# A two-layer graph and expert network on one core: input statistics, the epsilon and a bookkeeping part placed ahead of the choice of experts

## The chip, the cores and the metric

The kernel runs on 1 core of one Trainium2 chip. The metric is the device time of one execution in microseconds (us). Below, TensorE is PE in the profile, VectorE is DVE, ScalarE is ACT, GpSimd is POOL, and SP is the queue that issues most of the DMAs.

## The reference

The input `x` has 128 graphs of 64 nodes with 256 features (8192 rows in all), and `adj` holds a 64x64 matrix for each graph. All is float32. Two layers follow each other, and each has a graph part and an expert part. Cut to what matters here, the first layer is:

```python
# graph part of layer 0, on xn = layernorm(x)
agg = epsilon * xn + einsum('bnm,bmd->bnd', adj, xn)
h   = silu(rmsnorm(agg @ W1 + b1) * rms_weight)      # 256 -> 1024
x   = x + h @ W2 + b2                                # 1024 -> 256
# expert part of layer 0, on xn = layernorm(x)
top, idx = top_k(xn @ gate_w.T, 6)                   # 6 of 64 experts for each row
w   = softmax(top)
mix = sum over the 6 of w_k * (xn @ lattice[idx_k])  # each expert is a 256x256 matrix
x   = x + layernorm(xn + mix @ out_w.T + out_b)
```

The second layer has another graph part and 8 experts with a hidden layer of 512, of which each row uses 2.

## The kernel before

**Passes.** The program is a row of stages. The first pass computes the graph part of layer 0 and the routing of its experts; its scatters write each row, once for each of its six experts, into a table in DRAM that is ordered by expert. Then come the pages of the 64 experts, a second pass with the rest of layer 0 and the graph part of layer 1, and the pages of the 8 experts. The change lies in the first pass.

**Tiling.** A block is 256 rows, held as two tiles of 128 partitions; there are 32 blocks. The pass is a software pipeline. A list names pairs of a lag and a function, and `staggered` walks through it: in step s each function works on block s minus its lag, in the list's order. So in step s the hidden layer of block s is computed (lag 0), the input of block s+1 is normalised (lag -1), block s-2 gets its residual (lag 2), block s-3 is routed (lag 3), and the rest of the rows of block s-4 are sent (lag 4).

**What sets the order.** TensorE, VectorE and ScalarE run under a manual schedule: each executes its own instructions in the order in which the list emits them, one after the other, so an instruction that waits holds up all behind it on its engine. SP's DMAs are ordered by the framework. GpSimd issues the scatters in the order in which they are written.

**The functions of a step that the change and the prediction speak of.**

- `norm_a` (lag -1): the statistics of the input block, on VectorE, two pairs of L45 and L46 (one pair for each tile). They read the block that `load0` (lag -2, L620 for the rows and L574 for the adjacency) had loaded in an earlier step.
- `norm_e` (lag -1): adds epsilon times the unit matrix to the adjacency (L656, VectorE).
- `norm_s` (lag -1): the reciprocal root of that variance on ScalarE (L58 a logarithm, L59 an exponential). `norm_b` then normalises the block on VectorE (L666), and `aggregate` multiplies with the adjacency on TensorE (L674) and copies the result with ScalarE (L677).
- `residual_a` (lag 2): adds the input to the projected block (L723, VectorE) and takes the statistics of the sum (again L45 and L46). `residual_s` has the root of it (L58, L59, ScalarE). `residual_b` makes a small shift (L733, VectorE) and writes the normalised rows six times (L736, ScalarE); two DMAs store them (L738, L739).
- `hidden` (lag 0): four parts of the product with W1 on TensorE (L684), each followed by squares on ScalarE (L687). `square_sum` adds the squares (L694, VectorE), `rms` makes the mean with a matmul (L698) and its reciprocal root on ScalarE, and `scale` applies it (L706 on VectorE, L708 on ScalarE).
- `project` (lag 1): the product with W2 (L717, TensorE). `turn` and `gate` (lag 2): the transposes of the normalised rows (L76) and the logits of the 64 experts (L752).
- `choose` (lag 3): the six largest logits and a one-hot mark for each (L204 to L209, VectorE). `count` (lag 3) adds up the marks on TensorE (L217), `weigh` prepares the weights (L283 and L285 on VectorE, L286 on ScalarE), and `place` turns the counts into rows of the table (L300 to L327, VectorE).
- `keep_books` (lag 3, from block 4 on): the bookkeeping of the table's chunks on VectorE, spread over four steps (reach, grow, and two of note), and in each step in two parts, half 0 and half 1 (L228 to L267).
- `send` (lags 3 and 4): for each of the six ranks a weight on VectorE (L305) and two scatters by GpSimd (L334).
- `load_lattice` (lag 1): a load of expert matrices in some of the steps (L787).

In ScalarE's order of a step stand the squares of the first two hidden parts, the root of `residual_s`, the root of `norm_s`, the exponential of `weigh`, the squares of the other two hidden parts, the rows of L736, the copies of L677 and L746, and the root and the scaling of the hidden layer.

Of the kernel before, what the change touches and what calls it, by code (L numbers as in the profile page):

```python
# [485 lines left out]
def staggered(n, stages, first=0):  # L486

    for s in range(first + min(lag for lag, _ in stages), n + max(lag for lag, _ in stages)):
        for lag, f in stages:
            if first <= s - lag < n:  # L490
                f(s - lag)
# [3 lines left out]
def two_layer_gnn_moe_kernel(ctx: ExitStack, tc: tile.TileContext, a: dict, out: bass.AP):  # L495
# [84 lines left out]
    r0 = Router(tc, const, small, dram, N, D, E0, K0, T, P, 14 * P, 4, "r0", 3)  # L580
# [23 lines left out]
    with tc.tile_pool(name="c0", bufs=1) as c0, \  # L604
# [12 lines left out]
        def load0(b):  # L617
            B = blocks[b]
            B["x"] = x = x_view[:, b % 4 * T:(b % 4 + 1) * T, :]
            nc.sync.dma_start(out=x, in_=by_tile(x_in[ts(b, C), :]))  # L620
            B["at"] = load_adjacency(b)
# [57 lines left out]
        def hidden(b, j):  # L679
            B = blocks[b]  # L680
            B["ph", j] = ph = ph_pool.tile([P, 2, C], F32, name="ph")
            for c in range(2):
                for k in range(KD):
                    nc.tensor.matmul(ph[:, c, :], lhsT=w1[:, k, ts(2 * j + c, P)], rhs=B["aggT"][:, k, :],  # L684
                                     start=(k == 0), stop=(k == KD - 1))
            for c in range(2):
                nc.scalar.activation(sq[:, 2 * j + c, :], ph[:, c, :], AF.Square,  # L687
                                     bias=b1[:, 2 * j + c:2 * j + c + 1], scale=1.0)
# [87 lines left out]
        def send(b, k):  # L776

            B = blocks[b]
            r0.release(k, *B["w"], B["xs"])
            r0.send(B["row"], B["xs"], b > LOOK, (k,))  # L780

        def load_lattice(b):
# [5 lines left out]

        nc.scalar.preload_act_table_set("natural_log_exp_and_others")
        staggered(NB, (  # L790
            (3, choose),
            (3, lambda b: r0.keep_books(b, 0)),
            (2, residual_a),
            (4, lambda b: send(b, 2)),
            (-2, lambda b: load0(b) if b > 1 else None),
            (-1, norm_a),
            (0, lambda b: hidden(b, 0)),
            (0, lambda b: hidden(b, 1)),
            (2, residual_s),
            (-1, norm_s),  # L800
            (-1, norm_e),
            (4, lambda b: send(b, 3)),
            (3, weigh),
            (0, lambda b: hidden(b, 2)),
# [474 lines left out]
```

## Time and profile before

| what | us |
|---|---|
| median of 3 runs | 2058.91 |
| lowest and highest of them | 2055.96 and 2059.22 |
| the profiled execution | 2052.92 |
| its span, from the first instruction to the last | 2051.1 |
| TensorE's mean granted clock in it | 0.974 |
| the first pass in that span, to the last table scatter | 0 to about 645 |

The profile is of one execution. Its page gives the busy time of each engine and the span in 40 slices of 51 us, in tenths of busy time. The windows view gives the same sums for a chosen stretch. The list of waits says for each engine and line what it waited for, in total, how often, and the longest. The timeline gives each instruction's start and duration; a bracket after it is the idle time of the engine before it and what ended that. Where two neighbours on an engine don't depend on each other, the next one's start lies a little before the end of the one in front, so the time that an instruction takes out of its engine is read from start to start.

### The profile page before, as it was taken

To read this page: it belongs to the slowest core of one execution; us is meant where nothing else is said; L and a number is where in the kernel's file an instruction comes from. 1 tells how busy PE (TensorE), PEld (TensorE's weight loads), DVE (VectorE), ACT (ScalarE), POOL (GpSimd) and SP (SyncE) were. 2 spreads that over 40 slices of the span, in tenths; PEclk is the share of its full clock that TensorE was granted. 3 is DMA by queue.
4 is the path that set the end of the run, shared out by engine and by line. 5 is a ranking of instruction groups with operands and counts; after the bars stand their busy time and mean duration, and the time that the engine had idled before them with its cause. 6 is when DMAs were issued, how large, how long until landed. Compare 5 with 4: busy or idle time off the path is not lost. (4 is left out here: it accounts for less than half of the span.)

```text
span 2051.1 us, 37214 instructions
## 1 busy us (share of the span) xinstructions
PE 1923.0 (94%) x10516; PEld 1678.1 (82%) x10516; DVE 1200.0 (59%) x4205; ACT 1018.1 (50%) x2033; POOL 1162.0 (57%) x1134
## 2 busy tenths in 40 slices
PE   6999999999966989999999799999989999999996
PEld 5888888888865778888877688888868888888885
DVE  5899999999975333344333389999862222222221
ACT  4888888888851222222222266666643333333332
POOL 1377667677677777777777723333343444444443
PEclk9999999999977999999999899999989999999998
DMA  4244555544476988666665799888527766666664
GB/s 123 80 143 148 168 165 170 169 159 141 133 267 206 309 252 267 214 207 207 207 207 171 266 362 338 267 278 278 190 92 172 178 162 162 162 163 163 163 163 86
DMA packets 282561, 397.91 MB, mean 194 GB/s; under 512 B 56025, under 2 KB 236393, under 8 KB 282353
## 3 DMA queue, kind: packets, MB, share of 16 engines
q1 hardware_dynamic: 202880, 246.61, 40.2%
q0 software_dynamic: 64416, 136.14, 22.1%
q10 hardware_dynamic: 15056, 12.69, 1.9%
q8 instruction: 94, 1.54, 0.3%
q14 instruction: 115, 0.93, 0.2%
HBM read 222.84 MB, written 176.64 MB: 195 GB/s over the span
## 5 line engine op out<-in xcount | busy, mean ns | idle before, releaser
L334 POOL DMA_INDIRECT r0x<-xs,r0row x384 | 402.1, 1047 | 236.0 <-DVE lat L706 72.2
L341 POOL DMA_INDIRECT r0y<-px x404 | 393.3, 973 | 123.3 <-DMA r0y<-px 49.7
L918 PE MATMUL py<-lat,pxT 128*128 x1616 | 389.4, 384 | 18.7 <-ACT pxT L905 15.4
L351 POOL DMA_INDIRECT out_x<-py_s,px x138 | 214.6, 1555 | 293.8 <-DMA out_x<-py_s,px 125.9
L922 DVE TENSOR_SCALAR px<-py,px 128x256 f32<-128x256 f32 x404 | 177.0, 480 | 309.6 <-PE py L918 303.9
L918 PEld LDWEIGHTS py<-lat,pxT 128*128 128x128 f32 x1616 | 294.3, 192 | 59.3 <-ACT pxT L905 20.4
L905 ACT COPY pxT<-pt 128x512 f32<-128x512 f32 x202 | 117.9, 585 | 368.6 <-PE pt L903 252.7
L1217 ACT ACTIVATE phid<-ph,pw 128x256 f32<-128x256 f32 x276 | 130.6, 473 | 323.2 <-issue 213.9
L1215 PE MATMUL ph<-pxT,pw 128*128 128x256 f32 x1104 | 251.3, 381 | 0.7 <-ACT pxT L1206 0.7
L1235 PE MATMUL py<-fw,phid 128*128 (+1 forms) x1104 | 249.7, 379 | 0.0
L717 PE MATMUL ps<-lat 128*128 128x256 f32 x1024 | 238.5, 382 | 0.0
L1215 PEld LDWEIGHTS ph<-pxT,pw 128*128 128x128 f32 x1104 | 210.9, 191 | 30.0 <-ACT pxT L1206 1.1
L684 PE MATMUL ph<-lat 128*128 128x256 f32 x1024 | 232.2, 386 | 2.7 <-DVE lat L706 2.0
L1235 PEld LDWEIGHTS py<-fw,phid 128*128 128x128 f32 x1104 | 204.5, 190 | 25.0
L684 PEld LDWEIGHTS ph<-lat 128*128 128x128 f32 x1024 | 195.1, 193 | 29.4 <-issue 2.4
L334 POOL DMA_INDIRECT r1x<-xs,r1row x128 | 127.7, 998 | 160.9 <-DVE r1run L313 47.0
L717 PEld LDWEIGHTS ps<-lat 128*128 128x128 f32 x1024 | 193.8, 192 | 24.9
L1229 DVE TENSOR_SCALAR p<-p 128x2 f32<-128x2 f32 x69 | 12.8, 186 | 225.5 <-ACT p L1228 225.5
L1238 DVE TENSOR_TENSOR py_s<-py,pb 128x512 f32<-128x512 f32 x69 | 47.7, 692 | 154.9 <-PE py L1235 152.7
L903 PE MATMUL pt<-ident,px 128*128 128x128 f32 x808 | 125.3, 276 | 11.6 <-DMA px<-r0x 11.3
L903 PEld LDWEIGHTS pt<-ident,px 128*128 128x128 f32 x808 | 100.4, 142 | 37.7 <-DMA px<-r0x 8.9
L994 PE MATMUL ps<-ident,y 128*128 128x128 f32 x768 | 94.7, 281 | 16.1 <-DMA y<-r0y 16.1
(303 smaller groups left out, 2980.4 us busy)
## 6 DMA issues: line engine op xcount, KB each, us to landing
px<-r0x SPq DMA_DIRECT2D x404, 129.0 KB
y<-r0y SPq DMA_DIRECT2D x64, 768.0 KB
pw<-in_L_ffn_W1b SPq DMA_DIRECT2D x69, 514.0 KB
px<-r1x SPq DMA_DIRECT2D x69, 258.0 KB
x<-x SPq DMA_DIRECT2D x64, 256.0 KB
pb<-in_L_ffn_b SPq DMA_DIRECT2D x69, 128.0 KB
r0x<-r0filler ACTq DMA_DIRECT2D x64, 129.0 KB
lat<-in_x SPq DMA_DIRECT2D x32, 256.0 KB
```

Source lines behind the costliest of these rows:

```text
L334: i = self.nc.gpsimd.indirect_dma_start(out=self.table[:, :], out_offset=bass.IndirectOffsetOnAxis(ap=row[:, t, k:k + 1], axis=0), in_=xs[ ...
L341: d = self.nc.gpsimd.indirect_dma_start(out=self.answer[:, :], out_offset=bass.IndirectOffsetOnAxis(ap=x[:, self.D:self.D + 1].bitcast(I32 ...
L351: i, d = f"{self.name}add{i}", self.nc.gpsimd.indirect_dma_start(out=self.total[:, :], out_offset=bass.IndirectOffsetOnAxis(ap=x[:, self.D ...
L684: nc.tensor.matmul(ph[:, c, :], lhsT=w1[:, k, ts(2 * j + c, P)], rhs=B["aggT"][:, k, :], start=(k == 0), stop=(k == KD - 1))
L717: nc.tensor.matmul(B["po"][:, t, :], lhsT=B["hT"][:, c, ts(t, P)], rhs=w2[:, c, :], start=False, stop=(t == T - 1 and c == KH - 1))
L903: nc.tensor.transpose(pt[:, k, ts(q, P)], Q["px"][:, q, ts(k, P)], ident)
L905: nc.scalar.copy(xT[:, :, :n * P], pt[:, :, :n * P])
L918: nc.tensor.matmul(py[:, q, :], lhsT=xT[:, k, ts(q, P)], rhs=lat[:, ds(regs["e"][(2 * j + q) % 4], 1), k, :].rearrange("p o d -> p (o d)") ...
L922: nc.vector.tensor_scalar(px[:, q, :D], py[:, q, :], px[:, q, D + 1:D + 2], None, op0=ALU.mult)
L1215: nc.tensor.matmul(ph, lhsT=w[:, k * F1 + c * P:k * F1 + (c + 1) * P], rhs=Q["xT"][:, k, :], start=(k == 0), stop=(k == KD - 1))
L1217: nc.scalar.activation(hid[:, c, :], ph, AF.Relu, bias=w[:, KD * F1 + c:KD * F1 + c + 1], scale=1.0)
L1235: nc.tensor.matmul(py[:, t, :], lhsT=Q["hid"][:, c, ts(t, P)], rhs=fw2[:, ds(e, 1), c, :].rearrange("p o d -> p (o d)"), start=(c == 0), s ...
```

## The change

In the list of the first pass three entries change their place. `norm_a` and `norm_e`, which stood behind `residual_a`, now stand at the head of the list, and the first half of `keep_books` now stands ahead of `choose` instead of behind it. The functions themselves are as they were, and so are all other entries. On VectorE a step's order is now the input's statistics, the epsilon, the first bookkeeping part, the choice of experts and then the residual, where it was the choice, the bookkeeping, the residual, the input's statistics and the epsilon.

```diff
         nc.scalar.preload_act_table_set("natural_log_exp_and_others")
         staggered(NB, (
+            (-1, norm_a),
+            (-1, norm_e),
+            (3, lambda b: r0.keep_books(b, 0)),
             (3, choose),
-            (3, lambda b: r0.keep_books(b, 0)),
             (2, residual_a),
             (4, lambda b: send(b, 2)),
             (-2, lambda b: load0(b) if b > 1 else None),
-            (-1, norm_a),
             (0, lambda b: hidden(b, 0)),
             (0, lambda b: hidden(b, 1)),
             (2, residual_s),
             (-1, norm_s),
-            (-1, norm_e),
             (4, lambda b: send(b, 3)),
             (3, weigh),
             (0, lambda b: hidden(b, 2)),
```

## The prediction

> **What bounds the kernel now.** I number the turns of the first pass by the block whose hidden layer they compute (step 17 is that of block 17). First the page, for the engines' shares and for the stretch of the pass, which its first 11 to 12 slices hold:
>
> ```profile
> PE 1923.0 (94%) x10516; PEld 1678.1 (82%) x10516; DVE 1200.0 (59%) x4205; ACT 1018.1 (50%) x2033; POOL 1162.0 (57%) x1134
> ...
> DVE  5899999999975333344333389999862222222221
> ...
> PEclk9999999999977999999999899999989999999998
> ```
>
> The 59% of VectorE (DVE) is an average: in the pass it shows 9s. The windows view of steps 7 to 30 (us; busy and count of PE, PEld, DVE, ACT, POOL; granted clock; DMA share; GB/s), and who waits there:
>
> ```profile
> 133.00:565.00 432.00, 422.42 (x2385) 370.82 (x2385) 410.47 (x1390) 364.41 (x700) 302.21 (x288) 1.00 0.47 156
> ```
> ```profile
> ACT rstd L58 <- DVE xs L305: 26.9, 24, 1.9
> ...
> ACT rstd L58 <- DVE bn_mv L46: 14.3, 24, 0.6
> PE ps L76 <- ACT lat L677: 9.6, 17, 1.6
> ...
> DVE lat L694 <- ACT lat L687: 2.2, 7, 0.5
> ...
> DVE xs L283 <- issue: 0.5, 3, 0.2
> ```
>
> In 432 us VectorE waits 2.7 us in all; the rest of what it isn't busy lies between dependent instructions. TensorE (PE) waits 9.6, always before the transposes of L76 for ScalarE (ACT), which waits for statistics of VectorE. So from step 7 on the chain goes through VectorE, and TensorE is nearly as full. The timeline, from the end of one step's eighth L706 to the next, gives the step's length by its bookkeeping part: 17.90 (reach), 18.66 (grow), 17.50 and 17.50 (note): all with VectorE unbroken. Steps 3 to 6, without bookkeeping, take 17.35 to 17.56; there VectorE waits 0.86 to 1.41 before L694, and TensorE doesn't wait.
>
> The timeline of step 17 (start us, us, engine line; what waited in brackets):
>
> ```profile
> 317.70 0.18 DVE L46 BATCH_NORM_AGGREGATE bn_mv<-bn_st 128x2 f32<-128x6 f32 x1
> ...
> 317.85 0.42 DVE L45 BATCH_NORM_STATS2 bn_st<-lat 128x6 f32<-128x256 f32 x1
> 317.92 0.30 ACT L58 ACTIVATE rstd<-bn_mv,eps 128x2 f32<-128x2 f32 x1 [0.98 <-DVE xs L305]
> ...
> 318.93 0.39 DVE L656 TENSOR_TENSOR at<-at,eye 128x256 f32<-128x256 f32 x1
> ...
> 319.05 0.30 ACT L58 ACTIVATE rstd<-bn_mv,eps 128x2 f32<-128x2 f32 x1 [0.59 <-DVE bn_mv L46]
> ...
> 319.24 0.15 DVE L305 TENSOR_TENSOR xs<-r0w,r0den 128x2 f32<-128x2 f32 x1
> ...
> 319.61 0.94 DVE L666 TENSOR_SCALAR lat<-lat,bn_mv,rstd 128x256 f32<-128x256 f32 x2
> ...
> 319.70 1.55 ACT L687 ACTIVATE lat<-ph,c_L_gnn_b 128x256 f32<-128x256 f32 x4
> ...
> 321.28 2.41 DVE L694 TENSOR_TENSOR lat<-lat 128x1024 f32<-128x1024 f32 x3 [0.20 <-ACT lat L687]
> ```
>
> The reader is to see two relays. The residual's statistics end at 317.88 and ScalarE starts their root (L58, L59) 0.04 later. While it does, VectorE takes the input's statistics and epsilon, 317.85 to 319.24; ScalarE then roots those too, and L666 starts at 319.61, just 0.04 after that root's end. ScalarE's work is hidden under VectorE's.
>
> **The change part by part.** No instruction is added or removed; the built order shows TensorE's and GpSimd's (POOL's) as they were, ScalarE's the same but for buffer names.
>
> *Input statistics and epsilon ahead.* Two L45, two L46 and L656 take 319.24 - 317.85 = 1.39 us from start to next start. They now run before the choice, and the residual's statistics end 1.39 later: 319.27 in step 17. But ScalarE's order is as before, the residual's root first and the input's behind it. The input's statistics lie ready and wait in line. Step 2 shows both roots back to back, from the first L58 to the L666 that they release:
>
> ```profile
> 51.62 0.31 ACT L58 ACTIVATE rstd<-bn_mv,eps 128x2 f32<-128x2 f32 x1
> ...
> 52.62 0.73 DVE L666 TENSOR_SCALAR lat<-lat,bn_mv,rstd 128x256 f32<-128x256 f32 x2 [0.26 <-ACT rstd L59]
> ```
>
> That is 1.00. L666 so starts at 319.27 + 0.04 + 1.00 = 320.31 instead of 319.61: **0.70 later**. VectorE has only L305, L305, L283 and L285 to fill the time and then stands at L733 and L666. The squares of L687, 0.13 after the second root before, also move 0.70, to 320.40. Behind L666 on VectorE wait the sends' weights, the second bookkeeping part, L694 (released by those squares), the placing and the scaling; behind the squares on ScalarE L736, L677 and, on TensorE, the transposes of L76, which wait 0.28 already in this step. Nothing on this way has slack, so the step grows by 0.70. The terms are the same at step 16 (grow): L46 ends at 300.03, L666 starts at 301.76, and would start at 300.03 + 1.39 + 1.04 = 302.46.
>
> Steps 7 to 30: 24 x 0.70 = 16.8. In steps 19, 21 and 25 VectorE lost up to 0.19 at L283 and ScalarE up to 0.28 at L286, which now fall into the wait: minus 3 x 0.25 = 0.75. Steps 3 to 6: in step 6 the residual's statistics end at 120.23, the second root would end at 120.23 + 1.39 + 0.96 = 122.58, the squares run 122.71 to 124.3 instead of ending at 123.86 (they waited 0.16 for TensorE): 0.44 each, 1.8 in four. Step 2: ScalarE is busy until 51.6 anyway, nothing. **Sum: 16.8 - 0.75 + 1.8 = 17.8 us.**
>
> The Trainium skill ("VectorE: DVE Perf Modes", "The DRAIN you can't avoid") says that a next operation doesn't start until the pipe is empty, and that one which is not held starts earlier. By its first sentence the five instructions would cost their full times, 0.42 + 0.18 + 0.39 + 0.18 + 0.39 = 1.56, the delay would be 0.87, and the sum 22.6. The row decides for 1.39: L45 follows the L46 in front of it 0.10 after its start, not 0.18.
>
> *First bookkeeping part ahead of the choice.* It stands before the residual in both orders, so it moves no statistics. The choice's result (L209) comes later by 1.39 and the part's 0.4 to 1.2 us. In step 17 that is 315.69 + 1.79 = 317.48; its reader, the counting matmul, starts at 319.21 behind the hidden layer. In step 16 about 299.8 against 300.92. Hidden; without that cover it would cost what it is late.
>
> *DMAs and queues.* SP issues the next input (L620) when the residual has read the slot, so 1.39 later, with the store L738 behind it. Its reader is the next step's L45, now about 13.6 us after the issue instead of 19. The first input was issued at 0.74 and read at 7.76, so landing took at most 7.0: hidden. The adjacency loads (L574, up to four blocks ahead) change places with one store in five steps: hidden by three steps of lead. GpSimd's scatters of the third rank (L305 behind the residual) start 1.39 later in the step. Twelve of 0.97 + 0.30 make 15.3 us of 18.6, and it waited 53.4 us for L305 in these 24 steps: hidden, to the same lead.
>
> *The end of the pass.* From step 31 on no input is normalised, and the scatters run back to back:
>
> ```profile
> 565.68 0.97 POOL L334 DMA_INDIRECT r0x<-xs,r0row  x1 [1.76 <-ACT lat L708]
> ```
>
> GpSimd waits 1.76 there, so it carries no backlog that could swallow a late start: the tail and all behind it move by the whole 17.8.
>
> The profiled execution took 2052.92 (span 2051.1, 1.8 around it), 6.0 under the median of the three runs. 2052.9 + 17.8 = 2070.7; on the median's scale 2058.9 + 17.8 = **2076.7 us**.
>
> **The rivals.** A: *same mechanism, partly absorbed.* If TensorE's 17.35 us were as much the bound in all steps as in steps 3 to 6, each would lose 0.44: 28 x 0.44 = 12.3, 2071.2. Against it: the steps of 17.50 to 18.66.
>
> B: *the clock falls.* TensorE's wait before L76 grows from 0 to 0.72, as it is mostly, to 0.7 to 1.4:
>
> ```profile
> 451.68 0.66 PE L76 MATMUL ps<-ident,xs 128*128 128x128 f32 x4 [1.63 <-ACT lat L677]
> ```
> ```profile
> 584.04 0.80 PE L217 MATMUL route<-r0hot,r0tri 128*128 128x128 bf16 x6 [3.35 <-DVE r0hot L209]
> ```
>
> After 1.63 the next 16 matmuls took 3.62 as ever; after 3.35 they took 5.73, and the counting 1.65 instead of 1.0: about 3 us lost. It decides at a wait between these two. In the six grow steps: 6 x 3 = 18 more, 2095.
>
> C: *faster.* If the choice waited for the gate's logits at a step's start, the moved work would fill that wait, up to 1.39 a step, less the 0.70: 28 x 0.69 = 19, 2039.6. It wins only where the gate ends more than 0.70 after VectorE is free. The gate ends at 312.41 in step 17, before the choice at 313.46, and even in step 6 to 7 0.18 before; no wait of the choice is listed.
>
> D: *no difference*: ScalarE's roots hidden by other work, 2058.9. It needs 1.04 us of work between the statistics and L733; there is about 0.5.
>
> **How the numbers follow.** Forecast 0.72, A 0.12, B 0.04, C 0.07, D 0.05. A measurement of this kernel tells some 0.2% (4.1 us) from no change; A, B and the forecast are slower: 0.88. The range: from A less the 3 us by which the runs differ, 2068, to a delay of 0.95 a step (the full 1.39 less 0.44 of cover), 28 x 0.95 = 26.6, 2085.5, and the runs' spread: 2087. It leaves out B, C and D.
>
> **What would show it.** Right: L733 or L666 waits for ScalarE's L59 in nearly every step from 7 to 30, steps of about 18.2, 18.2, 18.6 and 19.4, no 0.59 wait before the second L58, L76 waiting 0.7 to 1.4, and from step 31 on a plain shift. Wrong: VectorE unbroken there, clock below 1.00 in the pass, L45 waiting for a DMA, or the later stages changing their length.

## The result and the profile after

| what | before | after |
|---|---|---|
| median, us (4 runs each) | 2059.06 | 2075.17 |
| lowest and highest | 2055.96, 2059.88 | 2072.18, 2080.58 |
| the profiled execution | 2052.92 | 2080.58 |
| its span | 2051.1 | 2078.8 |
| step 26 (note), step 27 (reach), step 12 (grow) | 17.50, 17.92, 18.66 | 18.07, 18.46, 19.40 |
| end of step 30 (of its eighth L706) in the span | 564.9 | 581.4 |

The change makes the kernel slower: the ratio is 1.0084, with a 95% interval of 1.006 to 1.0108, 16.1 us between the medians; 2076.7 had been predicted. The profiled execution of after is the longest of its four, and that of before lies 6 us under its median. So the two spans, 27.7 us apart, show more than the change. A second profile of the changed kernel (the last group of experiments) has a span of 2066.7 and stands 15.7 above before's; where the two profiles of after differ, I say so. Ratios, here and below, are of executions that the chip did not slow down, so they can differ from the quotient of the medians by some tenths of a per cent.

The lines of the page of after that answer to those shown of before, engine shares and the slices:

```profile
PE 1924.2 (93%) x10516; PEld 1677.0 (81%) x10516; DVE 1201.7 (58%) x4205; ACT 1012.2 (49%) x2033; POOL 1175.1 (57%) x1134
...
DVE  5899999999985333444333389999862222222221
...
PEclk9999999999987999999999899999989999999998
```

Busy sums and counts hardly differ: the engines do the same work, and what was added is standing still. The windows view of after from 133 us, as before's, to the end of step 30 (length; busy and count of PE, PEld, DVE, ACT, POOL; granted clock; DMA share; GB/s), and its list of waits in steps 7 to 30 (us in total, times, longest). Step 7 starts at 136.8 here and at 133.6 before, so 3.2 of the 449.0 us belong to step 6; the 24 steps themselves take 444.6 us, and 431.4 before.

```profile
133.00:582.00 449.00, 426.55 (x2402) 373.70 (x2401) 415.77 (x1402) 362.38 (x705) 317.69 (x292) 1.00 0.45 150
```
```profile
ACT rstd L58 <- DVE xs L305: 61.6, 24, 3.2
...
PE ps L76 <- ACT lat L677: 22.2, 24, 1.7
...
DVE lat L666 <- ACT rstd L59: 6.3, 24, 0.3
DVE bn_nm L733 <- ACT rstd L59: 2.6, 17, 0.2
...
DVE lat L694 <- ACT lat L687: 1.7, 6, 0.3
```

Three things are to be seen. VectorE now stands before L666 in all 24 steps and before L733 in 17, both times for ScalarE's L59; before, neither wait was listed. The wait of the second L58 for L46 (14.3 us before) is gone, and the first L58 waits 61.6 us instead of 26.9, since the residual's statistics come later. TensorE waits before L76 in every step, up to 1.7, and the clock of the window is still 1.00. The timeline of step 17 of after, cut to the instructions shown of before's, with L285 and L286 besides:

```profile
322.50 0.15 DVE L305 TENSOR_TENSOR xs<-r0w,r0den 128x2 f32<-128x2 f32 x1
322.58 0.42 DVE L45 BATCH_NORM_STATS2 bn_st<-lat 128x6 f32<-128x256 f32 x1
...
323.66 0.39 DVE L656 TENSOR_TENSOR at<-at,eye 128x256 f32<-128x256 f32 x1
...
328.22 0.18 DVE L46 BATCH_NORM_AGGREGATE bn_mv<-bn_st 128x2 f32<-128x6 f32 x1
...
328.43 0.30 ACT L58 ACTIVATE rstd<-bn_mv,eps 128x2 f32<-128x2 f32 x1 [2.37 <-DVE xs L305]
...
328.68 0.16 DVE L285 TENSOR_TENSOR r0w<-r0top 128x12 f32<-128x12 f32 x1
...
328.87 0.28 ACT L58 ACTIVATE rstd<-bn_mv,eps 128x2 f32<-128x2 f32 x1
329.00 0.16 DVE L733 SCALAR_TENSOR_TENSOR bn_nm<-bn_mv,rstd 128x2 f32<-128x2 f32 x1 [0.15 <-ACT rstd L59]
329.18 0.20 ACT L59 ACTIVATE rstd<-rstd 128x2 f32<-128x2 f32 x1
329.29 0.20 ACT L286 ACTIVATE r0w<-r0w 128x12 f32<-128x12 f32 x1
...
329.39 1.55 ACT L687 ACTIVATE lat<-ph,c_L_gnn_b 128x256 f32<-128x256 f32 x4
329.42 0.73 DVE L666 TENSOR_SCALAR lat<-lat,bn_mv,rstd 128x256 f32<-128x256 f32 x2 [0.26 <-ACT rstd L59]
...
330.98 2.41 DVE L694 TENSOR_TENSOR lat<-lat 128x1024 f32<-128x1024 f32 x3 [0.28 <-ACT lat L687]
```

Counted from the step's first L305 (313.38 before, 322.50 after), the residual's last L46 ends at 5.90 instead of 4.50, L666 starts at 6.92 instead of 6.23, and L694 at 8.48 instead of 7.90. The input's statistics, done by 323.66, lie ready for 5 us, and their root still starts at 328.87, behind the residual's. Delays: 1.40, 0.69, 0.58.

In every one of the 24 steps the growth is the delay of L694: from its start to the end of the step nothing changes by more than 0.02. And L694's delay is smaller than L666's, for it waits for two things. One is the last of the squares on ScalarE, which end at 321.25 before and at 330.94 after; L694 starts 0.03 later in both. Between the second root and the squares stands `weigh`'s exponential, L286, which reads what VectorE's L285 writes. Its lines before:

```profile
319.38 0.16 DVE L285 TENSOR_TENSOR r0w<-r0top 128x12 f32<-128x12 f32 x1
...
319.58 0.21 ACT L286 ACTIVATE r0w<-r0w 128x12 f32<-128x12 f32 x1
```

Before, L285 ends at 319.54 and L286 starts 0.03 later, when the root has just ended (319.58); the squares start at 319.70, 0.12 after the root. After, L285 is done 0.45 ahead, L286 starts 0.09 before the root's end, and the squares start 0.01 after it. So the squares come 0.57 later where the root comes 0.69 later, and in the reach and note steps, where L694 starts 0.03 after the last square in both kernels, the step grows by that 0.57.

The other thing is VectorE's own work in front of L694. In the grow steps it is longer than the squares, and there is no wait at L694 before or after. There the duration of L666 counts: the two take 0.73 after, and took 0.94 before. The groups of L666 in steps 7 to 30, before and after (busy us, mean ns of one, idle before):

```profile
L666 DVE TENSOR_SCALAR lat<-lat,bn_mv,rstd 128x256 f32<-128x256 f32 x48 | 21.6, 492 | 0.0
```
```profile
L666 DVE TENSOR_SCALAR lat<-lat,bn_mv,rstd 128x256 f32<-128x256 f32 x48 | 17.6, 410 | 6.3 <-ACT rstd L59 6.3
```

The same instruction became 82 ns shorter on average, 3.9 us in 48. It is the second one of each pair that changed: 0.59 to 0.62 in 20 of the 24 steps before, 0.40 to 0.43 in the other four, and 0.40 to 0.41 in all after. With it VectorE gets to L694 0.13 to 0.28 ahead of the squares in the reach and note steps, where it is not what the growth hangs on.

### The profile page after: what moved, and what is told of

Its sections match the earlier page's. It is cut to its first block, busy times and chain, and to the rows that moved or that the text cites. A ratio compares the mean times of both kernels' runs of the same rounds, so it can differ in the third digit from the quotient of the medians.

```text
span 2078.8 us, 37244 instructions
## 1 busy us (share of the span) xinstructions
PE 1924.2 (93%) x10516; PEld 1677.0 (81%) x10516; DVE 1201.7 (58%) x4205; ACT 1012.2 (49%) x2033; POOL 1175.1 (57%) x1134
## 5 line engine op out<-in xcount | busy, mean ns | idle before, releaser
L334 POOL DMA_INDIRECT r0x<-xs,r0row x384 | 416.0, 1083 | 239.4 <-DVE lat L706 73.9
```

Source lines behind the costliest of these rows:

```text
L334: i = self.nc.gpsimd.indirect_dma_start(out=self.table[:, :], out_offset=bass.IndirectOffsetOnAxis(ap=row[:, t, k:k + 1], axis=0), in_=xs[ ...
```

## The experiments

The theory (S): the step grows because ScalarE takes the residual's root first, and the residual's statistics are late behind the moved ones; the input's root then waits in line, and L666 and the squares with it. Rivals: (R1) what costs is the choice and its mark, which come later, or the bookkeeping part in front of them; (R2) the shift has another carrier, such as the epsilon, the scatters or a DMA; (R3, rival C of the prediction) the choice waits for the gate, and moved work fills that wait. The expectations use letters of their own: B in e1 and e2 and C in e5 stand for R1, and D in e5 (the input's rows have not landed so early) belongs to R2. V in e6 to e8 says that the loss is VectorE's own, through the neighbours that its instructions have now.

Two of the chips run the kernel before itself at 2303 and 2337 us, so each ratio is to the kernel before on the same chip, and no time is compared across chips. The first eight kernels ran on these two, and none of them had the ratio that S gave for it; the part on rival C comes back to that. What they show of S is read from their steps.

| kernel | median us (runs) | before on that chip | ratio [95%] |
|---|---|---|---|
| e1_norm_only | 2278.88 (6) | 2303.35 (26) | 0.9889 [0.9842, 0.9936] |
| e2_books_only | 2294.67 (10) | 2303.35 | 0.9968 [0.9945, 0.999] |
| e4_stats_only | 2295.14 (10) | 2303.35 | 0.9971 [0.9939, 1.0002] |
| e5_between | 2283.19 (9) | 2303.35 | 0.9934 [0.9907, 0.9961] |
| e5_again | 2290.89 (10) | 2303.99 (19) | 0.9939 [0.9901, 0.9976] |
| e9_again | 2302.56 (10) | 2303.99 | 1.0003 [0.9962, 1.0043] |
| e6_roots_swapped | 2309.69 (4) | 2337.16 (19) | 0.9887 [0.9839, 0.9936] |
| e7_normalise_first | 2316.57 (4) | 2337.16 | 0.9891 [0.9842, 0.994] |
| e8_squares_first | 2336.62 (10) | 2337.16 | 0.9954 [0.9917, 0.9992] |
| e9_eps_on_gpsimd | 2335.25 (10) | 2337.16 | 0.9997 [0.9972, 1.0022] |
| after_again | 2074.72 (4) | 2057.27 (13) | 1.0093 [1.007, 1.0117] |
| e8_again | 2052.83 (10) | 2057.27 | 0.998 [0.9965, 0.9995] |

**How the slow chips are read.** Their steps 7 to 30 take 485 to 547 us, where before's take 431. VectorE waits up to some 8 us before L204 or L706 in many steps there. A step in which it waits at neither I call undisturbed. Undisturbed steps can be compared across chips: one kernel, e8, ran on both kinds, and its undisturbed steps on the slow chip took 17.11, 17.13, 17.12, 18.56 and 17.58 (steps 9, 13, 17, 24, 27), the same steps on the other chip 17.11, 17.12, 17.12, 18.55 and 17.58. Where ScalarE's squares waited long for TensorE, I leave the step out as well (in e8, four steps of 24.7 to 24.8 in which L666 or L694 then waited 1.8 to 6.5 us). Lengths in us, from the eighth L706 of a step to the next one's:

| step | before | e2 | e4 | e1 | e5, e5_again | after | after_again |
|---|---|---|---|---|---|---|---|
| 10 (note) | 17.50 | 18.25 | 17.75 | 18.17 | 18.16, 18.15 | 18.08 | 18.08 |
| 26 (note) | 17.50 | - | 17.75 | 18.08 | 18.15, 18.15 | 18.07 | 18.07 |
| 30 (note) | 17.50 | - | 17.75 | 18.08 | 18.15, 18.15 | 18.06 | 18.08 |
| 8 (grow) | 18.81 | 18.82 | 18.82 | - | 19.32, - | 19.27 | 19.29 |
| 12 (grow) | 18.66 | 18.83 | 18.85 | 19.18 | 19.16, 19.19 | 19.40 | 19.41 |
| 28 (grow) | 18.65 | - | 18.83 | 19.15 | -, 19.18 | 19.39 | 19.40 |

### One part of the change at a time

**e1_norm_only**: before, with the statistics and the epsilon moved to the head; the bookkeeping stays behind the choice.

```diff
+            (-1, norm_a),
+            (-1, norm_e),
             (3, choose),
             (3, lambda b: r0.keep_books(b, 0)),
             (2, residual_a),
             (4, lambda b: send(b, 2)),
             (-2, lambda b: load0(b) if b > 1 else None),
-            (-1, norm_a),
...
-            (-1, norm_e),
```

> Input statistics and epsilon stand at the head, the first bookkeeping part stays behind the choice. Theory S (the residual's statistics come 1.39 us later, and ScalarE's two roots, which stood one beside VectorE's work and one just behind it, are now both waited for): all of the loss, a ratio to before of 1.007 to 1.009, steps of 18.1, 18.1, 18.5 and 19.4 us. Rival B (the bookkeeping part in front of the choice, with the one-hot marks later still, is the cause): a ratio within 0.002 of 1.

**e2_books_only**: before, with the bookkeeping part alone ahead of the choice.

```diff
-            (3, choose),
             (3, lambda b: r0.keep_books(b, 0)),
+            (3, choose),
```

> Only the first bookkeeping part stands ahead of the choice. Theory S: no statistics move, ratio 0.998 to 1.002, steps as before (17.5, 17.5, 17.9, 18.7 us). Rival B: most of the 16 us, ratio 1.005 to 1.008.

**e4_stats_only**: before, with `norm_a` alone at the head; `norm_e` stays behind `norm_s`.

```diff
+            (-1, norm_a),
             (3, choose),
...
-            (-1, norm_a),
```

> Only the input's statistics stand at the head, the epsilon stays where it was. Theory S: the residual's statistics come 1.08 us later instead of 1.39, so the second root ends 0.39 later than before instead of 0.70; with L666 shorter by 0.16, as in the changed kernel, a step grows by 0.23 to 0.39: 6 to 10 us, ratio 1.003 to 1.005. A rival by which the loss comes from where the statistics stand, whatever lies behind them (the input not yet landed, or the late choice): nearly all of the 16 us, ratio 1.007 or more.

Measured: by time, e1 is 1.1% faster than before on its chip, e2 0.3%, and e4 can't be told from before. By its time, e1 speaks against S; I come back to that. By its steps, it carries all of S. Its note steps have after's length (18.08 against 18.06 and 18.07), with after's waits: its list of steps 7 to 30 has L733 and L666 waiting for ScalarE's root, which e2's has not but for a few stray ones. The lists of waits of e1 and, behind it, of e4:

```profile
DVE bn_nm L733 <- ACT rstd L59: 5.0, 17, 0.6
...
DVE lat L666 <- ACT rstd L59: 3.9, 15, 0.3
```
```profile
DVE lat L666 <- ACT rstd L59: 5.3, 20, 0.3
...
DVE bn_nm L733 <- ACT rstd L59: 3.2, 5, 1.1
```

In e4 the L656 stays behind the residual, so the residual's statistics come later by two pairs of L45 and L46 only: 1.08 by the rows of before's step 17 instead of 1.39, 0.31 less. L666 waits 0.26 in every undisturbed step, and the note steps take 17.75, 0.33 less than e1's 18.08 and 0.25 more than before's 17.50: a smaller delay gives a smaller growth, by what it is smaller. The grow steps agree: in 12 and 28 of e4 L666 starts 0.35 and 0.36 later than before's and the second L666 is 0.2 shorter, which leaves 0.16 of the 0.19 and 0.18 by which the steps are longer. That e4's 18.82 to 18.85 stand within 0.02 of e2's is chance: e2's step 12 is 0.17 longer than before's with both relays as in before, and 0.14 of that is L207, which takes 0.31 there and 0.17 in before. In e2's one undisturbed note step, L694 also waited 0.79, so its 18.25 is no measure of the bookkeeping.

Four of the six grow steps of the full change show 0.2 on top. With the statistics moved and the part left behind the choice (e1, e5) step 12 takes 19.16 to 19.19, and in the full change 19.40. In step 16 of after L207 takes 0.39 and L244 0.35, in before 0.17 and 0.20; over steps 7 to 30 these two lines take 0.8 and 0.6 us more than before. Only L207 costs a step anything: the instruction behind L244 starts 0.11 after it in both kernels, and L666 is 0.93 later in these steps instead of 0.69. Nor is it a price of the bookkeeping alone, for in e1, with the part left behind the choice, L207 is long in 13 of the 24 steps, step 16 (19.34) among them. The last section shows when it is long.

### Choice first, statistics still ahead of the residual

**e5_between** and, on another occasion, **e5_again**: before, with the statistics and the epsilon directly ahead of the residual, behind the choice and the bookkeeping.

```diff
             (3, choose),
             (3, lambda b: r0.keep_books(b, 0)),
+            (-1, norm_a),
+            (-1, norm_e),
             (2, residual_a),
             (4, lambda b: send(b, 2)),
             (-2, lambda b: load0(b) if b > 1 else None),
-            (-1, norm_a),
...
-            (-1, norm_e),
```

> The choice and its bookkeeping part stay first; the input's statistics and the epsilon stand between them and the residual. Theory S: the residual's statistics are as late as in the changed kernel, so all of the loss, ratio 1.007 to 1.009. Rival C (the choice of experts comes too late for the counting or the sends): the choice is as early as before, ratio within 0.002 of 1. Rival D (the input's rows have not landed that early in the step): the statistics are read 2 to 4 us later than in the changed kernel, so a good part of the loss goes.

> The choice and its bookkeeping part first, then the input's statistics and the epsilon, then the residual; once more, for a chip on which the kernel before takes some 2059 us. Theory S: the residual's statistics are as late as in the changed kernel, ratio 1.006 to 1.010, steps of 18.1, 18.1, 18.5 and 19.2 to 19.4 us. Rival C (the late choice is the cause): 0.998 to 1.002. Where the kernel before takes 2300 us or more: 0.990 to 0.996, as measured there.

Here the choice is as early as before, so R1 foresees before's steps, and S foresees after's. The undisturbed steps come near after's: 18.15 in note (after 18.07), 19.16 to 19.19 in grow (19.40), with L666 waiting 0.26 and L733 up to 0.16 in them. The list of waits of e5_again:

```profile
DVE bn_nm L733 <- ACT rstd L59: 7.7, 19, 1.3
...
DVE lat L666 <- ACT rstd L59: 4.2, 16, 0.3
```

A later choice is not what costs. It is the place of the statistics against the residual's, and R1 is out; the 0.2 of four grow steps is L207's.

### ScalarE's and VectorE's order mended

**e6_roots_swapped**: the changed kernel, with the input's root ahead of the residual's.

```diff
-            (2, residual_s),
             (-1, norm_s),
+            (2, residual_s),
```

> The changed kernel, with the input's root ahead of the residual's on ScalarE. Theory S: one root instead of two lies between the residual's statistics and L666; L733 and L666 come 0.26 us earlier than in the changed kernel (0.76 instead of 1.02 after those statistics), and the squares too. Steps of 17.8, 17.8, 18.2 and 19.1 us, ratio to before 1.004 to 1.006. Rival V (the loss is VectorE's own, from which neighbours its instructions have): no change from the changed kernel, 1.007 to 1.009.

**e7_normalise_first**: e6, and L666 ahead of L733 on VectorE.

```diff
-            (2, residual_b),
             (-1, norm_b),
+            (2, residual_b),
```

> As the run before, and the normalising (L666) stands ahead of the shift of the residual (L733) on VectorE, so that it fills the wait for the residual's root. Theory S: no wait at L733 or L666 is left; the squares of the last two hidden parts still start some 0.3 us later than in the kernel before, which only the two note steps feel at L694. Ratio 1.000 to 1.002. Rival V: still 1.005 or more.

**e8_squares_first** and, on the chip with the short times, **e8_again**: e7, and the third pair of squares ahead of the residual's root.

```diff
             (-1, norm_s),
+            (0, lambda b: hidden(b, 2)),
             (2, residual_s),
             (4, lambda b: send(b, 3)),
             (3, weigh),
-            (0, lambda b: hidden(b, 2)),
```

> As the run before, and the squares of the third hidden part stand ahead of both roots on ScalarE, where it waited 2 to 3 us. Theory S: the input's statistics stand as far ahead as in the changed kernel, and nothing is lost: VectorE unbroken from step 7 on, steps of 17.4, 17.4, 17.9 and 18.7 us, ratio 0.998 to 1.000. Rival V: 1.005 or more, as the order on VectorE is still nearly that of the changed kernel.

e6 had two undisturbed steps: 18.08 in step 19 (after 18.46, before 18.15) and 18.82 in step 16 (after 19.40, before 18.66). L666 no longer waits for its root, and L733 still waits 0.15 for the residual's, which is now the second. So these two steps are 0.38 and 0.58 shorter than after's with the order of two roots alone turned. In step 16 0.22 of that is L207, which takes 0.17 in e6; so the roots' order is worth some 0.37 in both, where 0.26 was expected. Before's step 19 holds waits of its own, 0.17 at L283 and 0.32 at L694; beside the 17.88 to 17.92 of its reach steps 11, 15 and 27, e6's has 0.18 of the growth left, and step 16 has 0.16. e7 had no undisturbed step: VectorE waited before L204 in all 24, and its steps tell nothing of S. Both are 1.1% faster than before on their chip, which S alone does not explain. e8_squares_first had five, shown above; its 0.5% to before is barely outside no difference, and the medians in the table differ by 0.5 us. Its expectation says that the third squares stand ahead of both roots; the edit puts them behind the input's root and ahead of the residual's.

### The changed kernel and e8 on the chip with the short times

> The changed kernel once more, because the chips of the last two sets ran the kernel before at 2303 and 2337 us and TensorE's semaphores told VectorE of the gate's end up to 5 us late. Where the kernel before takes some 2059 us: ratio 1.006 to 1.011 as at first. Where it takes 2300 us or more: the choice then waits for the gate, the moved work fills that wait (the prediction's rival C), and the ratio is 0.986 to 0.994, like that of the run that moved the statistics and the epsilon alone.

> The order with both roots and the third squares rearranged, once more. Theory S where the kernel before takes some 2059 us: VectorE unbroken from step 7 on, ratio 0.996 to 1.000. Rival V there: 1.005 or more. Where the kernel before takes 2300 us or more: 0.992 to 0.999, as measured before.

The changed kernel repeats its result: 1.0093 [1.007, 1.0117], steps as in the table, 445.0 us for steps 7 to 30 (before 431.4, the first profile of after 444.6). From the end of step 30 on it stands 14.6 above before, at the span's end 15.7: the later stages move, and keep their length to about 1 us. The other 12 us by which the first profile of after is longer, 1.8 of them up to the end of step 30 and most of the others behind the pages of the 64 experts, are not in this one, so they belong to the execution and not to the change.

e8_again is 0.2% faster than before, 0.998 [0.9965, 0.9995]. It keeps VectorE's moved statistics and the moved bookkeeping, and turns the sign with the order of ScalarE's roots and squares and of two lines of VectorE. Its timeline of step 17, roots, L666, squares and L694:

```profile
315.54 0.31 ACT L58 ACTIVATE rstd<-bn_mv,eps 128x2 f32<-128x2 f32 x1
315.88 0.20 ACT L59 ACTIVATE rstd<-rstd 128x2 f32<-128x2 f32 x1
...
318.05 0.29 ACT L58 ACTIVATE rstd<-bn_mv,eps 128x2 f32<-128x2 f32 x1 [1.23 <-DVE xs L305]
...
318.37 0.73 DVE L666 TENSOR_SCALAR lat<-lat,bn_mv,rstd 128x256 f32<-128x256 f32 x2
...
318.61 0.82 ACT L687 ACTIVATE lat<-ph,c_L_gnn_b 128x256 f32<-128x256 f32 x2
319.01 0.16 DVE L733 SCALAR_TENSOR_TENSOR bn_nm<-bn_mv,rstd 128x2 f32<-128x2 f32 x1
...
319.63 2.41 DVE L694 TENSOR_TENSOR lat<-lat 128x1024 f32<-128x1024 f32 x3
```

The input's root is done at 316.08, 2.3 before L666 needs it; the residual's root runs under the two L666; the last two squares end at 319.43, before L694. VectorE has no wait above 0.15 in any of steps 7 to 30: its steps take 17.12 (17) and 17.26 (18) in note, 17.58 in reach (19) and 18.80 in grow (16), 425.7 us in all. Step 30 ends 4.9 before before's. The L666 are short here too:

```profile
L666 DVE TENSOR_SCALAR lat<-lat,bn_mv,rstd 128x256 f32<-128x256 f32 x48 | 18.0, 417 | 0.0
```

From start to start that is 3.8 of the 5.7 us by which its 24 steps beat before's. Before's own waits of VectorE, 2.7 at L694 and L283, are gone too, and L207 takes 0.8 more: 3.8 + 2.7 - 0.8 = 5.7. The two profiled executions still end level (spans of 2051.2 and 2051.1), as e8's later stages are 5.0 longer; before's is one that lies 6.0 under its median.

So S stands: with the same instructions moved ahead on VectorE, the growth is there with ScalarE's order as it was, and gone with the input's root and a pair of squares ahead of the residual's root and L666 ahead of L733. Of these three moves only the first was tried by itself on the changed kernel (e6, two steps), and it took away most of it. R2 falls with it, for the epsilon, the scatters and the DMAs are moved in e8 as in after. Of V the 0.2 at L207 is left, which e8 has too (18.80 in those four grow steps).

**e9_eps_on_gpsimd** and **e9_again**: e8, and the epsilon's addition on GpSimd, to take 0.31 us of each step off VectorE.

```diff
-            nc.vector.tensor_add(at, at, eye.unsqueeze(1).to_broadcast([P, T, P]))
+            nc.gpsimd.tensor_add(at, at, eye.unsqueeze(1).to_broadcast([P, T, P]))
```

> As the run before, with the epsilon added by GpSimd instead of VectorE. Theory S with VectorE as the bound of steps 7 to 30: 0.31 us less in the reach and grow steps, and down to TensorE's 17.36 in the others: some 5 us faster than the run before, ratio 0.995 to 0.998. If GpSimd's scatters bound the step or slow VectorE down: no gain, 1.000 or more.

> The rearranged roots and squares, with the epsilon added by GpSimd, once more. VectorE as the bound of steps 7 to 30: up to 0.31 us less in a reach or grow step than in the run without GpSimd (17.6 and 18.8 us there), 3 to 6 us in all, ratio to before 0.995 to 0.998. If GpSimd's own work or its reads get in VectorE's way: no gain, 0.998 to 1.002. Where the kernel before takes 2300 us or more: within 0.004 of 1.

No gain in time on either slow chip (0.9997 and 1.0003). The addition takes 0.74 on GpSimd. The undisturbed steps of e9_again went both ways against e8_again: 16.77 (17.11) in step 9, 17.40 (17.26) in step 18, 17.21 (17.24) in step 26, 18.66 (18.55) in step 24. It was not run on the chip with the short times, where its worth stays open.

### Rival C on the slow chips

The prediction gave 7 in 100 to a choice that waits for the gate, and on two chips it does wait. The timeline of e2_books_only at the turn to step 15, and its list of waits ("remote": the profile names no instruction as the releaser):

```profile
310.11 1.00 PE L752 MATMUL rms_p<-m_L_ffn_gate_wT,xn1T 128*128 128x64 f32 x8
...
316.28 0.23 DVE L204 MAX8 r0top<-rms_p 128x8 f32<-128x64 f32 x1 [3.60 <-remote]
...
316.37 1.57 ACT L687 ACTIVATE lat<-ph,c_L_gnn_b 128x256 f32<-128x256 f32 x4 [2.63 <-remote]
```
```profile
DVE r0top L204 <- remote: 33.7, 10, 4.1
...
DVE r0top L204 <- PE ph L684: 8.3, 4, 3.1
```

The gate's matmuls end at 311.1 by the profile, and VectorE, which waits for them, starts at 316.28; ScalarE, which waits for matmuls behind these, at 316.37. TensorE's semaphore updates of that stretch stand at 315.49 and 316.26 to 316.58, five within 1.1 us. Such a wait is room that moved work can fill. e1 beside e2 on one chip fits that: 6.0 us of waits before L204 instead of 43.9, and steps 7 to 30 in 492.3 us instead of 503.8. But it doesn't explain the row of ratios. e4 waits as little before L204 (7.1) and is not faster than e2; it loses 58.1 before L706. e5, with the choice in before's place, waits 11.5 and 18.5. And e7 waits about 80, in all 24 steps, and is 1.1% faster than before. The kernel before has no profile on these chips, nor was the changed kernel run there. What the sign of the full change would be there, and why the updates come late, stays open.

## Why the prediction was right

**Right, with its numbers.** The residual's statistics came 1.40 later (1.39 predicted). L666 came 0.69 later (0.70), and waited for L59 in all 24 steps. The 0.59 wait ahead of the second L58 is gone. TensorE waits 0.5 to 1.7 before L76 (0.7 to 1.4 predicted). From step 31 on there is a shift and little else. The first bookkeeping part, the DMAs and the scatters were costed at nothing: e2 has no wait at L733 or L666 to speak of, no L45 waits for a DMA in after, and only the 0.2 that L207 adds in four grow steps was missed.

The Trainium skill's sentence on the empty pipe ("VectorE: DVE Perf Modes", "The DRAIN you can't avoid") would have made the first of these 1.56. The 1.40 sides with the row, and with what the same section says of an operation that is not held.

**The term that was mis-sized: 0.70 for each of the 24 steps.** They took 18.07 (note), 18.46 (reach) and 19.40 (grow), and grew by 0.57, 0.56 and 0.74 in most: 13.2 and 13.6 us in the two profiles, where 16.8 - 0.75 = 16.05 stood. The delay of L666 was right. What failed is "also move 0.70" for the squares: the 0.13 between the root and the squares was carried over, and it shrank to 0.01, since L286 no longer waits for VectorE. The squares of step 17 came 0.57 later, and 18 reach and note steps grew by 9.4 us instead of 11.85. The three steps with waits of their own did lose 0.26 to 0.29 less than their like (0.25 predicted). In the six grow steps "nothing on this way has slack" held, but not the durations: the second L666 was 0.2 shorter in all six and L207 0.2 longer in four, and they grew by 3.85 instead of 4.2. 9.4 + 3.85 is the 13.2 of the first profile.

**Steps 3 to 6.** 1.4 us instead of 1.8: step 3 did not grow (17.56 in both), the others by 0.44, 0.49 and 0.50.

**The median.** 16.1 us against 17.8, closer than the parts: steps 3 to 30 grew by 14.6 and 15.1 in the two profiles, about 3 under the sum, and about 1 us came from behind the pass, where only a shift was predicted. after_again's span, 15.7, splits into 13.6 (steps 7 to 30), about 1 up to step 6, and about 1 behind step 30.

**The rivals.** A asked for 0.44 a step, 12.3 in all, and the measured 14.6 to 15.1 lies about as far from that as from 17.8. By size alone A is not refuted; by its mechanism it is. TensorE waits before L76 in all 24 steps of after, so it is not the bound, and 19 steps grew by 0.54 to 0.74; of the other five, three had waits of their own before, and two are grow steps in which L207 was no longer than before. B: the longest wait before L76 was 1.7, and the window's granted clock is 1.00. It needed a wait near 3.35. The profile of before narrows the gap: behind a wait of 2.55 at 598.71 the counting took 0.49 and 0.50, as ever. D fell. C was refused for a reason that held on the chip of the profile, where no choice waited; it is a property of the run and not of the kernel, as e2's lines show.

## What to carry to other kernels

Making a result ready earlier gains nothing when its reader takes its inputs in a written order: ask first who stands ahead of it in the queue of the engine that reads it, and what the move makes late for that one. Here the cure was to move the reader with the result (input's root ahead of the residual's, its squares and L666 along), and the same move of VectorE's work went from 0.9% slower to 0.2% faster.

A delay is to be followed along every way that leads to the next meeting point: here VectorE's L694 waits for its own engine's work and for ScalarE's squares, and the squares moved 0.12 less than the root in front of them. And when a step's cost is a sum of start-to-start times, leave room for durations that change with what runs beside them; one line here was 0.2 us off in 20 of 24 steps.

## What the runs showed of the hardware that was not expected

**A VectorE instruction's time hangs on when it falls beside GpSimd's scatter.** The second L666 (128x256, float32) took 0.59 to 0.62 where a scatter's instruction had started 0.45 to 0.47 before it (20 steps of before), and 0.61 where one had started 0.45 before it (two steps of e8_again). It took 0.40 to 0.43 where one had started 0.25 or 0.64 to 0.66 before it (4 steps of before), 0.36 or 0.07 before it (e8_again), and in all 24 steps of after. The scatters around the pair of step 17, before and after:

```profile
319.48 0.97 POOL L334 DMA_INDIRECT r0x<-xs,r0row  x1 [0.30 <-issue]
```
```profile
328.72 0.97 POOL L334 DMA_INDIRECT r0x<-xs,r0row  x1 [1.29 <-DVE xs L305]
...
330.00 1.00 POOL L334 DMA_INDIRECT r0x<-xs,r0row  x1 [0.30 <-issue]
```

Before, it runs from 319.48 to 320.45, and the second L666 from 319.94 to 320.55; after, one ends at 329.69 and the next starts at 330.00, and the second L666 starts between, at 329.75. Overlap alone doesn't do it, since the four short ones of before and e8_again's lie under a scatter too. What goes with it is the phase. In steps 7 to 30 of all 14 profiles, 99 L666 started 0.44 to 0.66 after the start of a scatter, and every one ended 1.06 to 1.08 after that start, about 0.1 behind the end of the scatter's 0.97, whether this made it 0.41 or 0.63 long. The other 573 took 0.39 to 0.47. L207 (a copy with a change of type, 128x12) shows the same: 48 started 0.55 to 0.73 after a scatter's start and ended 0.94 to 0.95 after it, 0.22 to 0.40 long; of the other 288 all but one took at most 0.19. The cause was not tried.

**TensorE's results can be reported several us after their matmuls' modelled end.** On two chips a choice that waited started up to 7.3 and 7.6 us behind the gate's modelled end (e9_again and e8_squares_first), with several updates at once in the stretch shown of e2, at a mean granted clock of 0.93 to 0.95 against 0.97 to 0.98. The kernel before took 12 to 14% longer on them, and e1, a part of this change, came out 1.1% faster there, though its undisturbed steps were longer than before's. A difference of 1% in this kernel so holds for the chip on which it was measured.
